# Full TensorE products cut into side-by-side column tiles when narrow tiles ran before them (two-layer transformer block, one core)

## The chip, the cores and the metric

The kernel runs on one core of one Trainium2 chip. The metric is the device time of one execution in microseconds, taken over several runs; one further execution was recorded by the hardware profiler. All data are 32-bit floats.

## The reference

Two layers on an input of 2 sequences x 1024 tokens x 256 features, cut here to what is computed:

```python
# layer 0, attention: 16 query heads of 16, 8 key/value heads, rotary positions
q, k, v = x @ W_Q.T, x @ W_K.T, x @ W_V.T            # x is normalized
scores = einsum('bsdkg,btdk->bkgst', rope(q), rope(k)) / sqrt(256)
ctx = einsum('bkgst,btdk->bkgsd', softmax(scores), v)
attn = ctx @ W_O.T
# layer 0, feed-forward: weights are codes into a table of 16 values
w = lut[idx]                                          # gate, up: 688x256; down: 256x688
ffn = (silu(x @ gate.T) * (x @ up.T)) @ down.T
# layer 1, recurrence per head of 64 (4 heads)
state = (1 - w_t)[..., :, None] * state + k_t[..., :, None] * v_t[..., None, :]
y_t = einsum('bhi,bhij->bhj', r_t, state)             # then y @ Wout
# layer 1, mixture of experts: 8 experts of width 176, two a token, and a shared one of 352
probs = softmax(x @ gate_w.T); weights, selected = top_k(probs, 2)
out = shared(x) + sum over the two of weight * expert(x)
```

Norms, residual products and sums stand around these parts.

## The kernel before

Tokens lie 128 to a partition block (16 blocks) or in four column blocks of 512. Nearly all of the work is on TensorE (PE); VectorE (DVE) takes row maxima, multiplies and masks, ScalarE (ACT) evaluates exponentials and SiLU and copies out of PSUM, GpSimd (POOL) decodes the table weights and does the gathers.

**The order is written out by hand.** `ORDER` is a string of about 2,000 letters. Each letter pops the next step off the list of that letter (`steps`), and each step issues its instructions on all engines. So the order of every engine's queue is fixed by the string. At `>` the attention part ends and its PSUM banks are handed on.

**Three kinds of product**, by how much of the 128x128 array they use:

- *Row tiles*: the contraction is over 32 rows (one head), 128 columns. Scores are computed twice: `largest` (L309, "mx") for the row maxima that DVE reduces (L316), `weigh` (L343, L335, "sc") for the exponentials that ACT takes (L347). Four heads in four row tiles run side by side. In the recurrence `diagonal` (L1192) uses 64 rows, and the second half of `reads` (L1341) 64 rows by 64 columns.
- *Column tiles*: 128 rows, the output in 32 or 64 partitions. `gather` (L371 and L360, "cx") multiplies the exponentials with the values of four heads, in four tiles of 32 columns side by side. `logits` (L728) uses 32 columns, `level` (L1234, "lev"), `states` (L1304) and the first half of `reads` (L1330, "y") use 64.
- *Full products* and transposes: 128 x 128. Full products are `qkv` (L218), `project` (L413, "so"), `gate_up0` (L562, L544, "gu", "gt"), `down0` (L578, "d"), `weights_of_decays` (L633), the recurrence's `project` (L1138), `values` (L1165, "vp") and `result` (L1357), the shared expert's `gate_up_s` (L753, "gus") and `down_s` (L1057, "ds"), the routing's `rank` (L846, L847) and `ids` (L927, "who"), and the experts' `gate_up` (L993) and `down` (L1021).

The kinds alternate often. In attention (about 25 to 560 us) the string mixes m, w (row tiles), v (column tiles), and single steps of the others: transposes (h, j, l, y, p) and full products (f, q, and A, the feed-forward of layer 0). From 567 us on, layer 1's recurrence (r) is woven with the feed-forward, routing (o), the shared expert (s) and the experts (X, G, H, D).

`gate_up_s` works in three blocks of rows of the shared expert's 352: 128, 128 and 96. Its weights `wgs` are loaded on SP's queue (L1096). `ids` collects the token numbers of every expert tile: 16 steps, each fed by a comparison on DVE (L916).

Of the kernel before, what the change touches and what calls it, by code (L numbers as in the profile page):

```python
# [61 lines left out]
NFS = len(FS)  # L62

# [10 lines left out]
C_ALL = C_PRIO + NE  # L74

# [27 lines left out]
def attention(  # L103
    nc, tc, st, b0, small, singles, xs, xnT, s_sb, wlut, ident, epst,
# [24 lines left out]
    for k in range(4):  # L129
        nc.tensor.matmul(bank(f"none_{k}"), xnT[:, 0, 0:P], xnT[:, 0, 0:512], start=True, stop=True)  # L130
# [71 lines left out]
    def turn_x(t):  # L202

        ps = bank(f"xnTp_{t}")
        for kc in range(KC):
            for k in range(2):
                nc.tensor.transpose(
                    ps[:, (2 * kc + k) * P : (2 * kc + k + 1) * P], xns[t + k][:, ts(kc, P)], ident
                )
        nc.scalar.copy(xnT[:, :, t * P : (t + 2) * P], ps.rearrange("p (k s) -> p k s", k=KC))  # L210
# [3 lines left out]
    def qkv(t):  # L214
        b, c = divmod(t, CPB)
        ps = bank(f"qkv_{t}")
        for kc in range(KC):
            nc.tensor.matmul(  # L218
                ps, xnT[:, kc, ts(t, P)], wqkv[:, kc, :], start=(kc == 0), stop=(kc == KC - 1)
            )  # L220
        qk = ps[:, 0:384].rearrange("p (h d) -> p h d", d=8)
        cs = att2.tile([P, 2, 2, HS, 8], F32, tag="cs", name=f"cs_{t}")
        nc.vector.tensor_tensor(
            cs.rearrange("p w a h d -> p w (a h) d"),
            qk.unsqueeze(1).to_broadcast([P, 2, 2 * HS, 8]),
            rope[:, :, c, :].unsqueeze(2).to_broadcast([P, 2, 2 * HS, 8]),
            ALU.mult,
        )
        nc.scalar.copy(vpads[b][:, c, :, 0:HD], ps[:, 384:512].rearrange("p (k d) -> p k d", d=HD))
        turned[t] = cs[:, 0], cs[:, 1]  # L230
# [17 lines left out]
    def turn_k(t):  # L248

        b, c = divmod(t, CPB)  # L250
        pk = bank(f"kTp_{t}")
        pkv = pk.rearrange("p (j k s) -> p j k s", j=2, k=2)
        for j in range(2):
            for k in range(2):
                nc.tensor.transpose(pkv[:, j, k, :], knat[(c + k) % 4][:, ts(j, 4), :], ident)
        nc.scalar.copy(kTs[b][:, :, c * P : (c + 2) * P], pk.rearrange("p (j s) -> p j s", j=2))
# [25 lines left out]
    def turn_q(tag, g, h):  # L282

        b, T = divmod(g, NQT)
        ps = bank(f"{tag}p_{g}_{h}")
        for c in range(BC):
            nc.tensor.transpose(ps[:, ts(c, P)], qns[b][:, T, BC * h + c], ident)
        qT = att2.tile([P, 512], F32, tag=tag, name=f"{tag}_{g}_{h}")
        nc.scalar.copy(qT, ps)
        qTs[tag, g, h] = qT  # L290

    def turn_first(c):

        if c == 0:
            qTs["qTb", 0, 0] = att2.tile([P, 512], F32, tag="qTb", name="qTb_0_0")
        ps = bank(f"qTbp_0_{c}_0")
        nc.tensor.transpose(ps[:, 0:P], qns[0][:, 0, c], ident)
        nc.scalar.copy(qTs["qTb", 0, 0][:, ts(c, P)], ps[:, 0:P])

    def largest(n, i):  # L300

        g, u = divmod(n, 16)
        b, T = divmod(g, NQT)
        c, half = divmod(u, 2)
        if (g, c) not in tops:
            tops[g, c] = att2.tile([P, 2, 4], F32, tag="top", name=f"top_{g}_{c}", bufs=4)
        at = slice(SLOT * i, SLOT * (i + 1))
        ps = bank(f"mx_{n}_{i}")
        nc.tensor.matmul(  # L309
            ps,  # L310
            qTs["qTa", g, c // BC][at, ts(c % BC, P)],
            kTs[b][at, T // 2, ts(half, 512)],
            start=True,
            stop=True,
        )
        nc.vector.tensor_reduce(tops[g, c][:, half, i : i + 1], ps, AX.X, ALU.max)  # L316
        done[g, c] = done.get((g, c), 0) + 1
        if done[g, c] == 8:
            top = tops.pop((g, c))

            nc.vector.tensor_reduce(
                qns[b][:, T, c, :, HD], top.rearrange("p h i -> p i h"), AX.X, ALU.max
            )

    def weigh(n, i):

        g, u = divmod(n, 16)
        b, T = divmod(g, NQT)
        h, c = divmod(u, 8)
        at = slice(SLOT * i, SLOT * (i + 1))  # L330
        ps = bank(f"sc_{n}_{i}")
        if n < 8:

            for k in range(4):
                nc.tensor.matmul(  # L335
                    ps[:, ts(k, P)],
                    kTs[0][at, 0, ts(c % 2 * 4 + k, P)],
                    qTs["qTb", 0, 0][at, ts(c // 2, P)],
                    start=True,
                    stop=True,  # L340
                )
        else:
            nc.tensor.matmul(  # L343
                ps, kTs[b][at, T // 2, ts(c, P)], qTs["qTb", g, h][at, :], start=True, stop=True
            )
        e = att2.tile([P, 512], F32, tag="e", name=f"e_{n}_{i}", bufs=EB)
        nc.scalar.activation(e, ps, AF.Exp, scale=1.0 / math.sqrt(E))  # L347
        es[n, i] = e

    def gather(n):  # L350
# [6 lines left out]
        if n < 8:  # L357
            for k in range(4):
                for i in range(4):
                    nc.tensor.matmul(  # L360
                        cxs[0, 0][SLOT * i : SLOT * (i + 1), ts(c // 2, P)],
                        values(0, c % 2 * 4 + k, i),
                        es[n, i][:, ts(k, P)],
                        start=(c % 2 == 0 and k == 0),
                        stop=(c % 2 == 1 and k == 3),
                    )
        for i in range(4):
            if n < 8:
                es.pop((n, i))
                continue  # L370
            nc.tensor.matmul(  # L371
                cxs[g, h][SLOT * i : SLOT * (i + 1), :],
                values(b, c, 4 * (T // 2) + i),
                es.pop((n, i)),
                start=(c == 0),
# [7 lines left out]
    def divide(g, h):  # L383
# [4 lines left out]
        for c in range(BC):  # L388
            nc.tensor.transpose(ps[:, ts(c, P)], ct[:, ts(c, P)], ident)
# [11 lines left out]
    def turn_c(t):  # L401
        ps = bank(f"cTp_{t}")
        for kc in range(KC):
            nc.tensor.transpose(ps[:, ts(kc, P)], s_sb[:, t, ts(kc, P)], ident)
# [4 lines left out]
    def project(t):  # L409
        cT = cTs.pop(t)  # L410
        po = bank(f"so_{t}")
        for kc in range(KC):
            nc.tensor.matmul(  # L413
# [28 lines left out]
def two_layer_kernel(  # L442
# [69 lines left out]
    def transpose_block(srcs, name):  # L512

        ps = bank2(name)
        for kc in range(KC):
            for k, s in enumerate(srcs):
                nc.tensor.transpose(ps[:, kc, ts(k, P)], s[:, ts(kc, P)], ident)
# [3 lines left out]
    singles = []  # L521
    ffw = ctx.enter_context(ExitStack())
# [16 lines left out]
    def gate_up0(n, f, which):  # L539
        if f == FB:  # L540

            ps = bank1(f"gt0_{n}")
            for kc in range(KC):
                nc.tensor.matmul(  # L544
# [16 lines left out]
        for kc in range(KC):  # L561
            nc.tensor.matmul(  # L562
# [11 lines left out]
    def down0(n, k):  # L574
        t = n * BC + k
        po = bank1(f"d0_{t}")
        for f in range(NF0):
            nc.tensor.matmul(  # L578
# [23 lines left out]
    def late_loads(part):  # L602
# [8 lines left out]
        nc, tc, att, b0, small, singles, xs, xnT, s_sb, wlut, ident, epst,  # L611
# [16 lines left out]
    def weights_of_decays():  # L628
        ps = bank1("wxwp")
        psv = ps.rearrange("p (k d) -> p k d", k=KC)  # L630
        for kc in range(KC):
            for k in range(KC):
                nc.tensor.matmul(  # L633
# [21 lines left out]
    singles.clear()  # L655
    more_hidden(ffw.enter_context(tc.tile_pool(name="h1", bufs=1, side="right")))
# [19 lines left out]
    wgs = shp.tile([P, KC, 2 * SH_CH], F32, name="wgs")  # L676
# [47 lines left out]
    def logits(n):  # L724
        ps = bank1(f"logits_{n}")
        for kc in range(KC):
            for k in range(BC):
                nc.tensor.matmul(  # L728
                    ps[SLOT * k : SLOT * (k + 1), 0:P],
                    gate[:, kc, :],  # L730
                    xnT[:, kc, ts(n * BC + k, P)],
                    start=(kc == 0),
# [15 lines left out]
    def gate_up_s(n, f):  # L748
        lo, sz = FS[f]
        ps = bank2(f"gus_{n}_{f}")  # L750
        for which in range(2):
            for kc in range(KC):
                nc.tensor.matmul(  # L753
                    ps[:sz, which, :],
                    wgs[:, kc, which * SH_CH + lo : which * SH_CH + lo + sz],
# [32 lines left out]
    def top_two(n):  # L788
# [3 lines left out]
        def turn_l():  # L792
            ps = bank1(f"lgp_{n}")
            nc.tensor.transpose(ps[:, 0:P], lgT[n], ident)
# [18 lines left out]
    def route():  # L813
# [29 lines left out]
        def rank():  # L843
            flat = both.rearrange("p c e -> p (c e)")
            ps = bank1("rank")
            nc.tensor.matmul(ps[:, 0:P], before, flat, start=True, stop=True)  # L846
            nc.tensor.matmul(ps[:, P : 2 * P], all1, flat, start=True, stop=True)  # L847
# [75 lines left out]
        def ids(c):  # L923
            if c == 0:
                whop.append(bank1("who"))
            for k in range(2):
                nc.tensor.matmul(  # L927
# [46 lines left out]
    def turn_x(i):  # L974
        ps = bank1(f"xgTp_{i}")
        xg = tiles.pop(("x", i))
        for kc in range(KC):
            nc.tensor.transpose(ps[:, ts(kc, P)], xg[:, ts(kc, P)], ident)
# [7 lines left out]
    def gate_up(i):  # L986
# [5 lines left out]
        for kc in range(KC):  # L992
            nc.tensor.matmul(  # L993
                ps[:, 0 : 2 * EI],
                xT[:, kc, :],
                late["gu"][:, kc, bass.ds(e * (2 * EI), 2 * EI)],
                start=(kc == 0),
# [10 lines left out]
    def turn_h(i):  # L1008
        ps = bank1(f"hgTp_{i}")
        h = tiles.pop(("h", i))  # L1010
        for k in range(2):
            nc.tensor.transpose(ps[:EH, ts(k, P)], h[:, ts(k, EH)], ident)
# [4 lines left out]
    def down(i):  # L1017
        ps = bank1(f"dne_{i}")
        e, hT = tiles.pop(("e", i)), tiles.pop(("hT", i))
        for k in range(2):  # L1020
            nc.tensor.matmul(  # L1021
                ps[:, 0:E],
                hT[:, k, :],
                late["d"][:, k, bass.ds(e * E, E)],
                start=(k == 0),
# [23 lines left out]
    def down_s(n, k, m):  # L1049
# [5 lines left out]
        for c in range(m):  # L1055
            for f, (lo, sz) in enumerate(FS):
                nc.tensor.matmul(  # L1057
# [75 lines left out]
    def project(n, what_):  # L1133
        wt = {"a": wxw, "r": w1[:, :, 0, :], "k": w1[:, :, 1, :]}[what_]
        pp = bank2(f"{what_}p_{n}")
        for m in range(KC):
            for kc in range(KC):
                nc.tensor.matmul(  # L1138
# [19 lines left out]
    def values(n, k):  # L1158
# [4 lines left out]
        for k2 in range(2):  # L1163
            for kc in range(KC):
                nc.tensor.matmul(  # L1165
# [15 lines left out]
    def diagonal(n, m):  # L1181
# [7 lines left out]
        for c in range(BC):  # L1189
            for par in range(2):  # L1190
                at = half(par)
                nc.tensor.matmul(  # L1192
# [13 lines left out]
    def level(n, lev):  # L1206
# [11 lines left out]
        for c in range(BC):  # L1218
            for pr in range(KC):
                for hf in range(2):  # L1220
# [10 lines left out]
                    else:  # L1231
                        continue
                    w_ = P if m == HALF else HALF
                    nc.tensor.matmul(  # L1234
                        ps[half(at), w_ * q : w_ * (q + 1)], kd[:, pr, src], to, start=True, stop=True
# [45 lines left out]
    def turn_k(n):  # L1281
        kd = B_[n, "k"]
        pt = bank2(f"kTp_{n}")
        for c in range(BC):
            for m in range(KC):
                nc.tensor.transpose(
# [8 lines left out]
    def states(n):  # L1295
# [4 lines left out]
        for c in range(BC):  # L1300
            for m in range(KC):
                for par in range(2):
                    ch = slice(P * m + 64 * par, P * m + 64 * (par + 1))
                    nc.tensor.matmul(  # L1304
                        puv[half(par), c, m, :], ke[:, c, ch], v[:, c, ch], start=True, stop=True
# [16 lines left out]
    def reads(n):  # L1322
# [3 lines left out]
        for c in range(BC):  # L1326
            for m in range(KC):
                for par in range(2):
                    ch = slice(P * m + 64 * par, P * m + 64 * (par + 1))
                    nc.tensor.matmul(  # L1330
                        pyv[half(par), m, c, :],
                        v[:, c, ch],
                        w[:, c, m, par, :],
                        start=(c == 0),
                        stop=False,
                    )
        for c in range(BC):
            for m in range(KC):
                for par in range(2):
                    at = half(par)  # L1340
                    nc.tensor.matmul(  # L1341
# [10 lines left out]
    def result(n, k):  # L1352
        po = bank1(f"s1_{n}_{k}")
        pov = po.rearrange("p (k d) -> p k d", k=2)
        for k2 in range(2):
            for m in range(KC):
                nc.tensor.matmul(  # L1357
# [110 lines left out]
def _arrays(i):  # L1468
# [27 lines left out]
    gs = np.concatenate([i["L1_ffn_shared_gate"], i["L1_ffn_shared_up"]], axis=0)  # L1496
# [43 lines left out]
```

## Time and profile before

| | us |
|---|---|
| median of 3 runs | 968.42 |
| lowest, highest | 968.21, 970.19 |
| the profiled execution | 968.03 |
| its span, from the first to the last instruction | 966.2 |

| stretch | what runs | PE busy | DVE busy |
|---|---|---|---|
| 0 to 100 us | norms, qkv, attention begins | 97.26 of 100 | 83.46 |
| 200 to 300 us | attention | 100.00 of 100 | 73.93 |
| 500 to 567 us | end of attention, feed-forward | 67.00 of 67 | 9.52 |
| 567 to 745 us | feed-forward, recurrence, routing, shared expert | 176.47 of 178 | 109.38 |
| 745 to 905 us | experts, recurrence | 159.40 of 160 | 74.40 |

How to read it: an engine's busy time is the union of its instructions' durations. Matmuls are pipelined, so the durations of neighbours overlap, and the time that a matmul costs the next one is the difference of their starts. "PEld" is the load of the stationary operand, which may run beside a matmul. A row of the timeline merges neighbouring instructions of one line and shape: start, length, engine, line, operation, output<-inputs, rows*columns of the array, and the count.

### The profile page before, as it was taken

What the parts mean: (1) busy time and instruction counts of PE and PEld (TensorE: products, weight loads), DVE (VectorE), ACT (ScalarE), POOL (GpSimd) and SP (SyncE); (2) the same over time, 40 slices, a digit from 0 to 9 for tenths busy, and PEclk for the clock granted to TensorE, in tenths of its full rate; (3) what the DMA queues carried; (4) which work ended last, traced back from release to release, by engine and by line L of the source; (5) the groups of instructions that cost most, each with busy time, mean ns of one, the idle gap of its engine ahead of it and who ended that gap; (6) DMA issues with size and microseconds to landing.
All of it is one profiled execution on the core that took longest, in us unless ns stands there. A gap on an engine that the chain in (4) does not pass through costs nothing.

```text
span 966.2 us, 17253 instructions
## 1 busy us (share of the span) xinstructions
PE 946.4 (98%) x6716; PEld 521.3 (54%) x6716; DVE 612.9 (63%) x1228; ACT 533.6 (55%) x1009; POOL 586.9 (61%) x485
## 2 busy tenths in 40 slices
PE   9999999999999999999999999999999999999976
PEld 4685433343334443443445475756457678777765
DVE  6998886877767766765760134467777634641795
ACT  4556856566675775766677545526313553464223
POOL 8999999999999999999912030202002345553244
PEclk9999999999999999999999999999999999999999
DMA  5000000000000000000000031002600122221142
GB/s 177 2 2 13 1 12 2 1 13 1 12 2 1 12 1 13 1 1 1 1 1 1 1 124 40 25 1 77 191 1 26 47 67 66 67 80 53 56 141 95
DMA packets 17864, 34.53 MB, mean 36 GB/s; under 512 B 2893, under 2 KB 11231, under 8 KB 17439
## 3 DMA queue, kind: packets, MB, share of 16 engines
q1 hardware_dynamic: 13527, 21.96, 7.2%
q0 software_dynamic: 3968, 10.80, 3.6%
q8 instruction: 54, 0.88, 0.4%
q10 hardware_dynamic: 288, 0.66, 0.2%
q14 instruction: 27, 0.22, 0.1%
HBM read 22.01 MB, written 11.40 MB: 35 GB/s over the span
## 4 chain that ended last, share of the span: by engine, by line
PE 93%; DVE 4%; issue 1%; POOL 1%; ACT 0%; POOLq 0%; ACTq 0%; DVEq 0%
PE sc L343 15%; PE mx L309 14%; PE cx L371 12%; PE gu L562 7%; PE gue L993 5%; PE d L578 4%; PE gus L753 4%; PE dne L1021 3%; PE qkv L218 3%; PE lev L1234 3%; PE sc L335 2%; PE so L413 2%; PE rp L1138 1%; PE vp L1165 1%; PE kp L1138 1%
## 5 line engine op out<-in xcount | busy, mean ns | idle before, releaser
L316 DVE TENSOR_REDUCE top<-mx 128x1 f32<-128x512 f32 x512 | 325.9, 684 | 100.1 <-PE mx L309 66.3
L347 ACT ACTIVATE e<-sc 128x512 f32<-128x512 f32 x512 | 271.7, 605 | 133.3 <-PE sc L343 61.4
L309 PE MATMUL mx<-kT,qTa 32*128 32x512 f32 x1024 | 282.7, 625 | 0.3 <-DVE top L316 0.3
L270 POOL TENSOR_SCALAR pick<-idx,lut 128x544 f32<-128x544 int32 x120 | 252.4, 2103 | 11.3
L343 PE MATMUL sc<-qTb,kT 32*128 32x512 f32 x960 | 254.8, 624 | 0.0
L274 POOL TENSOR_TENSOR wlut<-wlut,pick 128x544 f32<-128x544 f32 x120 | 160.5, 1337 | 10.0
L309 PEld LDWEIGHTS mx<-kT,qTa 32*128 32x128 f32 x1024 | 102.5, 183 | 63.3 <-DVE top L316 23.7
L343 PEld LDWEIGHTS sc<-qTb,kT 32*128 32x128 f32 x960 | 93.5, 183 | 76.6 <-DVE top L316 24.4
L371 PE MATMUL cx<-e,vpad 128*32 128x512 f32 x960 | 123.9, 603 | 0.0
L588 POOL TENSOR_TENSOR sgt<-s_sb,g 128x256 f32<-128x256 f32 x16 | 11.6, 728 | 154.0 <-ACT g L586 154.0
L966 POOL DMA_INDIRECT xg<-xn_h,who x39 | 39.4, 1009 | 94.8 <-PE s L1357 70.2
L1034 POOL DMA_INDIRECT y_h<-ye,who x39 | 39.8, 1021 | 69.3 <-ACT ye L1029 23.8
L562 PE MATMUL gu<-xnT,wlut 128*128 128x512 f32 x160 | 72.8, 598 | 0.0
L371 PEld LDWEIGHTS cx<-e,vpad 128*32 128x32 f32 x960 | 20.8, 108 | 84.1 <-issue 72.8
L1005 DVE TENSOR_TENSOR sge<-sge,gue 128x176 f32<-128x176 f32 x39 | 13.1, 338 | 73.4 <-ACT sge L1004 73.1
L572 DVE TENSOR_TENSOR h<-sg,gu 128x512 f32<-128x512 f32 x20 | 13.8, 688 | 65.5 <-ACT sg L571 50.3
L993 PE MATMUL gue<-wgu,xT 128*128 x156 | 53.0, 462 | 1.5 <-issue 0.9
L562 PEld LDWEIGHTS gu<-xnT,wlut 128*128 128x128 f32 x160 | 29.2, 190 | 34.0 <-issue 29.9
L578 PE MATMUL d<-wlut,h 128*128 128x256 f32 x192 | 44.1, 381 | 0.5 <-ACT s_sb L416 0.5
L753 PE MATMUL gus<-xnT,wgs 128*128 128x512 f32 (+1 forms) x96 | 43.1, 598 | 0.0
L1021 PE MATMUL dne<-wd,hTe 88*128 x156 | 40.0, 381 | 0.5 <-ACT hTe L1014 0.5
L578 PEld LDWEIGHTS d<-wlut,h 128*128 128x128 f32 x192 | 35.7, 190 | 8.1 <-issue 1.8
(235 smaller groups left out, 1330.3 us busy)
## 6 DMA issues: line engine op xcount, KB each, us to landing
xn_h<-xn SPq DMA_DIRECT2D x16, 256.0 KB, 3.6
yk<-y_h SPq DMA_DIRECT2D x16, 256.0 KB, 2.9
wgu<-in_wgu SPq DMA_DIRECT2D x1, 2816.0 KB, 10.3
idx<-in_idx SPq DMA_DIRECT2D x8, 272.0 KB, 2.8
out_x<-g SPq DMA_DIRECT2D x16, 128.0 KB, 1.7
wd<-in_wd SPq DMA_DIRECT2D x1, 1408.0 KB
xs<-in_x SPq DMA_DIRECT2D x2, 512.0 KB, 5.0
w<-in_w SPq DMA_DIRECT2D x1, 1024.0 KB
```

The lines of the kernel that those rows point to most:

```text
L270: nc.gpsimd.tensor_scalar(dst, codes[piece], float(j), lut[:, j : j + 1], ALU.is_equal, ALU.mult)
L274: nc.gpsimd.tensor_tensor(wlut[:, at], wlut[:, at], dst, ALU.add)
L309: nc.tensor.matmul(ps, qTs["qTa", g, c // BC][at, ts(c % BC, P)], kTs[b][at, T // 2, ts(half, 512)], start=True, stop=True,)
L316: nc.vector.tensor_reduce(tops[g, c][:, half, i : i + 1], ps, AX.X, ALU.max)
L343: nc.tensor.matmul(ps, kTs[b][at, T // 2, ts(c, P)], qTs["qTb", g, h][at, :], start=True, stop=True)
L347: nc.scalar.activation(e, ps, AF.Exp, scale=1.0 / math.sqrt(E))
L371: nc.tensor.matmul(cxs[g, h][SLOT * i : SLOT * (i + 1), :], values(b, c, 4 * (T // 2) + i), es.pop((n, i)), start=(c == 0), stop=(c == CPB ...
L562: nc.tensor.matmul(hT0[which], wlut[:, lo + kc * P :][:, 0:P], xnT[:, kc, ts(n, 512)], start=(kc == 0), stop=(kc == KC - 1),)
L578: nc.tensor.matmul(po[:, 0:E], hidden(n)[:, f, ts(k, P)], wd0[:, f, :], start=(f == 0), stop=(f == NF0 - 1),)
L753: nc.tensor.matmul(ps[:sz, which, :], wgs[:, kc, which * SH_CH + lo : which * SH_CH + lo + sz], xnT[:, kc, ts(n, 512)], start=(kc == 0), s ...
L993: nc.tensor.matmul(ps[:, 0 : 2 * EI], xT[:, kc, :], late["gu"][:, kc, bass.ds(e * (2 * EI), 2 * EI)], start=(kc == 0), stop=(kc == KC - 1),)
L1021: nc.tensor.matmul(ps[:, 0:E], hT[:, k, :], late["d"][:, k, bass.ds(e * E, E)], start=(k == 0), stop=(k == 1),)
```

## The change

A small class now issues the products and keeps the width of the last column tile in `form` (SLOT is 32, HALF 64, P 128):

```diff
+class Array:
+    def __init__(self, nc, narrow):
+        self.nc, self.narrow, self.form = nc, narrow, None
+
+    def rows(self, out, lhsT, rhs, start=True, stop=True):
+        self.form = None
+        self.nc.tensor.matmul(out, lhsT, rhs, start=start, stop=stop)
+
+    def matmul(self, out, lhsT, rhs, start, stop, width=None):
+        if len(lhsT.shape) > 2:
+            lhsT = lhsT.rearrange("p a b -> p (a b)")
+        w = self.form = width or self.form or self.narrow
+        for i in range(0, out.shape[0], w):
+            self.nc.tensor.matmul(out[i : i + w], lhsT[:, i : i + w], rhs, start=start, stop=stop)
+
+    def transpose(self, out, in_, ident):
+        self.form = P
+        self.nc.tensor.transpose(out, in_, ident)
```

All products go through it. Row tiles (L309, L335, L343, L1192, L1341) call `te.rows`, transposes call `te.transpose`, and the others call `te.matmul`. Column tiles give their own width, so they are issued as before; the experts' two products and the first four dummy products (L130) give `width=P` and stay full. The rest of the full products give none: each becomes four instructions of 32 columns, two of 64, or stays one, by what was issued last.

```diff
+    te = Array(nc, SLOT)
...
     go(">")
     att.close()
     singles.clear()
+    te.narrow, te.form = HALF, None
...
-        nc.tensor.matmul(
+        te.rows(
             ps,
             qTs["qTa", g, c // BC][at, ts(c % BC, P)],
             kTs[b][at, T // 2, ts(half, 512)],
...
-            nc.tensor.matmul(
+            te.matmul(
                 cxs[g, h][SLOT * i : SLOT * (i + 1), :],
                 values(b, c, 4 * (T // 2) + i),
                 es.pop((n, i)),
+                width=SLOT,
                 start=(c == 0),
...
-            nc.tensor.matmul(
+            te.matmul(
                 ps, xnT[:, kc, ts(t, P)], wqkv[:, kc, :], start=(kc == 0), stop=(kc == KC - 1)
             )
...
-                nc.tensor.matmul(
+                te.matmul(
                     whop[0][:, 0:NTILE],
                     at[c][:, k, :],
                     inside[:, 2 * c + k, :],
...
-            nc.tensor.matmul(
+            te.matmul(
                 ps[:, 0 : 2 * EI],
                 xT[:, kc, :],
                 late["gu"][:, kc, bass.ds(e * (2 * EI), 2 * EI)],
+                width=P,
```

The third block of `gate_up_s`, 96 rows wide before, is computed 128 wide, so that tiles divide it; its weights get 32 columns more, of zeros at the end, and the extra rows of the product are not read.

```diff
+SH_PAD = NFS * P - SH_CH
...
-    wgs = shp.tile([P, KC, 2 * SH_CH], F32, name="wgs")
+    wgs = shp.tile([P, KC, 2 * SH_CH + SH_PAD], F32, name="wgs")
...
-                nc.tensor.matmul(
-                    ps[:sz, which, :],
-                    wgs[:, kc, which * SH_CH + lo : which * SH_CH + lo + sz],
+                te.matmul(
+                    ps[:, which, :],
+                    wgs[:, kc, which * SH_CH + lo : which * SH_CH + lo + P],
                     xnT[:, kc, ts(n, 512)],
```

`ORDER`, the tiles, the pools and all instructions of the other engines are unchanged.

## The prediction

> **What bounds the kernel now.** I read the page first: busy shares and the chain of work that ended last.
>
> ```profile
> span 966.2 us, 17253 instructions
> PE 946.4 (98%) x6716; PEld 521.3 (54%) x6716; DVE 612.9 (63%) x1228; ACT 533.6 (55%) x1009; POOL 586.9 (61%) x485
> PE   9999999999999999999999999999999999999976
> PE 93%; DVE 4%; issue 1%; POOL 1%; ACT 0%; POOLq 0%; ACTq 0%; DVEq 0%
> ```
>
> TensorE (PE) is busy in every slice but the last two, and 93% of the closing chain is its own matmuls. So a saving on PE is worth its length almost everywhere, and only the end needs another look. A busy PE need not be streaming, though, so the second view is the timeline of TensorE, where differences of start times count (durations overlap).
>
> ```profile
> 98.86 1.07 PE L371 MATMUL cx<-e,vpad 128*32 128x512 f32 x8
> 99.86 1.99 PE L218 MATMUL qkv<-wqkv,xnT 128*128 128x512 f32 x4
> 101.77 1.07 PE L371 MATMUL cx<-e,vpad 128*32 128x512 f32 x8
> ...
> 576.30 13.90 PE L562 MATMUL gu<-xnT,wlut 128*128 128x512 f32 x32
> 590.12 0.64 PE L728 MATMUL logits<-xnT,gate 128*32 128x128 f32 x16
> ```
>
> The pair before the types is rows*columns of the array in use: 128*128 is a full product, 128*32 a tile of 32 columns, 32*128 a tile of 32 rows (mx, sc). One call shows as two matmuls, "passes" below (gu has 80 calls and 160 matmuls). A long run of full passes takes (590.12 - 576.30 = 13.82) / 32 = 0.43 us each. Four narrow ones run side by side: cx x8 is two rounds of four. But 99.86 to 101.77 is 1.91 us for four full passes worth 4 x 0.429 = 1.72, and cx x8 takes 1.00 us for two rounds worth 0.86. The rest, 0.19 and 0.14 us, is lost at changes of shape.
>
> From the starts of single matmuls that loss has two parts. **The change**: first start of the new shape less the last start of the old and its streaming time lies between 85 and 105 ns at 375 of the 390 changes, whatever the pair of shapes; I use 95. **The entry**: the second pass of the new shape comes later than in a steady run, by 104 ns for full products of 256 to 512 columns (533 against 429), 55 for transposes, 21 for the 39-column "who", 105 for row tiles, 24 for four narrow tiles (453 against 429), 50 for two.
>
> **The change, part by part.** I went through the 6,716 matmuls in order of start and gave each the shape that the new rule gives it (a row-tile product clears the form, a transpose sets it to full, a narrow product sets its width, a full product takes the form it finds, or 32, later 64, where there is none). Of the 988 full-product passes 116 become four tiles of 32 columns, 340 two tiles of 64, 532 stay full, all those behind a transpose among them.
>
> Changes of shape: 390 before, 360 after. The 30 fewer save 30 x 95 = 2.85 us.
> Entries before: 34 full products at 104, 61 transposes at 55, 3 "who" at 21, 111 four-tile at 24, 33 two-tile at 50, 4 of 64*64 at 50, 144 row tiles at 105: 26.6 us. After: 3, 68, 0, 115, 26, 4 and 144: 23.4 us. That saves 3.16 us. Transposes are entered seven times more, because a narrow product ahead of one now has to be left.
> Together 6.0 us: 2.8 before 567 us, 1.4 from 567 to 745, 0.3 from 745 to 905, 1.5 after it.
>
> **A saving on short products.** Weight loads bound small passes:
>
> ```profile
> 730.23 1.08 PE L927 MATMUL who<-inside,at 128*128 128x39 f32 x8
> 731.24 1.97 PE L1330 MATMUL y<-w,v 128*64 128x128 f32 x32
> 733.14 0.65 PE L1341 MATMUL y<-rd,zero 64*64 64x128 f32 x8
> ...
> 618.57 1.16 PE L1234 MATMUL lev<-rd,kT 128*64 128x64 f32 x32
> 619.66 0.70 PE L1165 MATMUL vp<-w,x2T 128*128 128x256 f32 x2
> ```
>
> "who" takes 1.01 us for 8 passes, 112 ns each in the middle, though it streams only 39 columns. lev takes 1.09 us for 16 rounds of two tiles, 58 ns a round. 48 of the 64 "who" passes become rounds of two tiles, which no row shows with 39 columns. Bounds: 112 ns each (no gain), 58 as lev (gain 48 x 54 = 2.6 us). lev is the nearer row, having the same width of load. But the matches that feed "who" come from DVE one by one, and the x16 run near 727 us shows PE idle for them, so 1.6 us of the 2.6 is taken as reaching the end.
>
> **What the narrow passes cost.** A row shows four tiles of 32 columns in steady state: from cx x32 to cx x64 eight more rounds of 128 columns cost 1.88 - 1.01 = 0.87 us, 109 ns each, exactly a full pass of 128.
>
> ```profile
> 55.32 1.08 PE L360 MATMUL cx<-e,vpad 128*32 128x128 f32 x32
> 56.33 1.14 PE L309 MATMUL mx<-kT,qTa 32*128 32x512 f32 x8
> 57.40 1.96 PE L360 MATMUL cx<-e,vpad 128*32 128x128 f32 x64
> 59.28 0.71 PE L309 MATMUL mx<-kT,qTa 32*128 32x512 f32 x3
> ```
>
> y above does the same for two tiles: 1.90 us for 16 rounds, 109 each plus change and entry. Four or two tiles that read one and the same moving tile, and two tiles with 256 or 512 columns, are in no row. Bounds: nothing a pass (those two rows), or 24 ns a pass, the delay that the second round has behind an entry, if weights were never loaded ahead: 456 x 24 = 10.9 us. I take nothing, since the shortest of these rounds, 128 columns, already hides its loads.
>
> Issue was my next doubt. lev starts 32 matmuls in 1.09 us, 34 ns each, and the four of a cx round start within 21 ns. [...]
>
> **Edits at no cost.** 688 more matmuls and as many loads lengthen PE's instruction stream by a tenth; instruction fetching takes 0.4% of the DMA engines (queue q8), which covers it; uncovered, the rows above would show starved rounds. Semaphores: cx signals on the last matmul of its eight alone, so tiles should add none. The last block of gus widens from 96 to 128 columns; its load goes from 159 to 190 ns under a pass of 429. wgs grows by 32 KB on SP's queue (in front of msk and wds); the load is issued at 570 us and gus first runs at 657, so 87 us cover it. No step is moved.
>
> **What of it reaches the end.** Until 567 us PE waits for data in few places; POOL decodes weights until 488 us and the first "d" that needs all of them starts at 512, so 24 us of slack lie there. DVE is 65 to 83% busy in the 100 us windows. I count 2.5 of the 2.8. From 567 to 745: 1.3 of 1.4. From 745 to 905, PE 99.6% busy: 0.3. After 905 it is different:
>
> ```profile
> 905.00:940.00 35.00, 28.16 (x270) 22.73 (x269) 33.47 (x54) 6.01 (x15) 10.90 (x12) 1.00 0.37 118
> 940.00:944.00 4.00, 4.00 (x16) 3.30 (x15) 3.93 (x9) 1.14 (x3) 2.34 (x2) 0.57 0.32 104
> ```
>
> These are windows: PE, its loads, DVE, ACT, POOL, granted clock, DMA. The timeline of TensorE in them:
>
> ```profile
> 925.38 1.15 PE L1234 MATMUL lev<-rd,kT 128*64 128x64 f32 x32 [1.60 <-DVE kT L1247]
> 938.91 1.09 PE L1234 MATMUL lev<-rd,kT 128*64 128x128 f32 x16 [3.14 <-DVE kT L1247]
> 939.94 3.31 PE L1165 MATMUL vp<-w,x2T 128*128 128x256 f32 x8
> ```
>
> Until 940 us DVE is busy for 33.5 of 35 us and PE waits for it, so a faster ds or vp is only a longer wait: 0.2 of 1.5.
>
> Sum: 2.5 + 1.3 + 1.6 + 0.3 + 0.2 = 5.9 us. The profiled execution took 968.03 us (span 966.2, 1.8 around it), 0.4 under the median of 968.42; 968.03 - 5.9 = 962.1, and against the median **962.5 us**.
>
> **Rivals.**
> (1) Other engines take the gain. For: DVE above 70% in attention, matches behind "who". If attention keeps 0.8, 567 to 745 keeps 0.7 and "who" and the end nothing: 1.8 us with the 0.3, so 966.6. Against: at 375 of 390 changes the next shape follows at once, without a wait.
> (2) Narrow passes are slower. Mechanism: tiles that share one moving tile, or that cannot load ahead, pay 24 ns on each of 456 passes: 10.9 - 5.9 = 5.0 us slower, 973.4. It decides from 5.9 / 456 = 13 ns a pass. For: no row has shared moving tiles, and cx runs hold more than two rounds of 512 rarely. Against: where they do (303.58 us, x16), later rounds take 429.
> (3) More arrives. All of 2.8 and 1.4 and 2.6 and 0.3, 0.7 of the end, and the clock dip at 940.5 to 943.9 misses vp (3.31 us at half clock, 1.99 for the same eight passes at 926): 9.1 us, so 959.3. The dip follows an idle stretch of 3.14 us, which earlier ds passes lengthen; so it may as well stay. [...]
>
> **How the numbers follow.** Forecast 0.60, rival 1 0.14, rival 2 0.14, rival 3 0.12. A measurement of this kernel tells about 0.2%, 1.9 us, from no change. The forecast and rival 3 are faster (0.72), rival 1 lies within it (0.14), rival 2 is slower (0.14). The range runs from below rival 3, with "who" and attention in full, 957.5, to half-way into rival 2, at 17 ns a pass (456 x 17 = 7.8, less 5.9, 970.3).
>
> **What would show it.** In the new timeline, qkv between two cx at 99 us should be x16 matmuls of 128*32, with 8 rounds from the first cx to the next mx in 3.55 us instead of 3.91. gu behind cx should still take 0.43 a pass; 0.45 is rival 2. "who" should start pairs every 58 ns. At 567 us the same d should start 2 to 3 us earlier; if not, rival 1. The forecast is wrong if passes lengthen, if each tile signals or waits, or if the gain at 905 us is gone at the end.

## The result, and the profile after

The changed kernel takes 962.98 us (median of 4 runs, 962.56 to 963.91), the kernel before 969.12 on the same chip (4 runs, 968.21 to 970.19): a ratio of 0.9939, with a 95% interval of 0.9927 to 0.9951. The forecast was 962.5. The profiled execution took 962.75 us, 5.28 less than the one before.

The page of the changed kernel, its span, busy shares and chain of waits:

```profile
span 961.0 us, 18629 instructions
PE 939.6 (98%) x7404; PEld 499.9 (52%) x7404; DVE 615.0 (64%) x1228; ACT 533.7 (56%) x1009; POOL 586.8 (61%) x485
PE 93%; DVE 5%; issue 1%; POOL 1%; ACT 0%; POOLq 0%; ACTq 0%; DVEq 0%
```

688 matmuls more (7,404 against 6,716), as counted, and still the same bound: TensorE (PE) busy for 98%. TensorE's busy time fell by 6.8 us, but that number can't say why. The timeline of TensorE can (L88 issues row tiles, L95 all other products, L99 transposes):

```profile
99.11 1.06 PE L95 MATMUL cx<-e,vpad 128*32 128x512 f32 x8
100.00 1.90 PE L95 MATMUL qkv<-wqkv,xnT 128*32 128x512 f32 x16
101.71 1.04 PE L95 MATMUL cx<-e,vpad 128*32 128x512 f32 x8
102.69 0.69 PE L88 MATMUL sc<-qTb,kT 32*128 32x512 f32 x1
...
722.84 2.24 PE L95 MATMUL who<-inside,at 128*128 128x39 f32 x16 [0.34 <-DVE at L946]
725.01 1.15 PE L95 MATMUL add<-v,ke 128*64 128x64 f32 x32
725.99 0.62 PE L95 MATMUL who<-inside,at 128*64 128x39 f32 x16
726.43 1.95 PE L95 MATMUL y<-w,v 128*64 128x128 f32 x32
...
933.59 1.50 PE L95 MATMUL lev<-rd,kT 128*64 128x128 f32 x16 [3.21 <-DVE kT L1279]
934.87 3.22 PE L95 MATMUL vp<-w,x2T 128*64 128x256 f32 x16
938.14 1.09 PE L99 MATMUL kTp<-cst,kT 128*128 128x128 f32 x8
```

Before, the row tiles behind the second cx started here:

```profile
102.77 0.69 PE L343 MATMUL sc<-qTb,kT 32*128 32x512 f32 x1
```

Three things are to be seen. The qkv that stood between two cx as x4 of 128*128 is now x16 of 128*32, and from the first cx to the next sc 3.58 us pass, where it was 3.91 (98.86 to 102.77; 3.55 forecast): both changes of shape are gone, and four qkv rounds take 1.71 us, 0.43 each. The narrow who takes 0.44 us for eight rounds from its start to that of y, where it took 1.01 us before, a change of shape included. And near the end TensorE still waits 3.21 us for DVE ahead of the last lev, and vp still runs at half clock (3.22 us; the window 934.0 to 937.5, shown under "Fillers", has a granted clock of 0.52).

Over the whole trace the count of changes of shape is 360 (390 before), as forecast. Of these, 348 still cost 85 to 105 ns by the prediction's measure (375 of the 390 before). Rounds of four tiles start every 429 ns at 512 columns and every 216 at 256, rounds of two every 429, 216 and 58 at 512, 256 and 39 columns (medians), as full passes of 512 and 256 columns did. The tiles signal no more often than the full products did: qkv 16 times and gu 28 times in both traces.

**Where the time came from.** A matmul that both kernels issue in the same shape is a landmark: its start before less its start after is the lead of the changed kernel. The table has the starts of five landmarks in the traces of all kernels run, in us: the first row tile of attention (mx), the first transpose of layer 1 (x1Tp), a transpose of an expert's tokens (xgTp), the last of the experts' products (dne) and a product of the recurrence near the end (lev).

| kernel | first mx | first x1Tp | third tile's xgTp | last tile's dne | last lev of 128 columns | end |
|---|---|---|---|---|---|---|
| before | 25.64 | 572.83 | 746.31 | 908.69 | 938.91 | 966.24 |
| changed | 25.88 | 570.84 | 741.23 | 903.27 | 933.59 | 960.97 |
| all full | 26.86 | 574.12 | 747.70 | 910.07 | 940.30 | 968.85 |
| attention only | 25.85 | 570.77 | 744.35 | 906.73 | 936.97 | 964.39 |
| layer 1 only | 26.81 | 574.09 | 744.43 | 906.47 | 936.80 | 965.26 |
| always narrow | 25.90 | 574.79 | 746.59 | 908.62 | 938.92 | 966.16 |
| who full | 26.08 | 571.01 | 743.37 | 905.42 | 935.75 | 964.00 |
| ds full | 26.88 | 571.80 | 742.11 | 904.15 | 934.41 | 961.08 |
| with fillers | 26.08 | 570.96 | 741.32 | 903.35 | 933.69 | 960.18 |
| best | 26.66 | 571.41 | 740.83 | 902.87 | 933.17 | 959.64 |

Until the first mx only full products and transposes run, and they are issued alike in all kernels but "always narrow" and "best". Still the first column scatters by 1.2 us. Most of that is there already behind the dummy products, whose eight passes took 5.53 us before and 6.76 in "all full". So leads below are counted from the first mx. The changed kernel gains 2.23 us to x1Tp (1.99 and the 0.24 of a later start), 3.09 from there to xgTp, 0.34 from there to dne, and gives back 0.15 by the end. With the 0.24 of the start that is 2.23 + 3.09 + 0.34 - 0.15 - 0.24 = 5.27 of span.

### The profile page after: what moved, and what is told of

It reads as the page before. It is cut to its first block, busy times and chain, and to the rows that moved or that the text cites. A ratio compares the mean times of both kernels' runs of the same rounds, so it can differ in the third digit from the quotient of the medians.

```text
span 961.0 us, 18629 instructions
## 1 busy us (share of the span) xinstructions
PE 939.6 (98%) x7404; PEld 499.9 (52%) x7404; DVE 615.0 (64%) x1228; ACT 533.7 (56%) x1009; POOL 586.8 (61%) x485
## 4 chain that ended last, share of the span: by engine, by line
PE 93%; DVE 5%; issue 1%; POOL 1%; ACT 0%; POOLq 0%; ACTq 0%; DVEq 0%
PE sc L88 17%; PE mx L88 14%; PE cx L95 13%; PE gu L95 7%; PE gue L95 5%; PE d L95 4%; PE gus L95 4%; PE dne L95 3%; PE qkv L95 3%; PE lev L95 2%; PE so L95 2%; PE kp L95 1%; PE ap L95 1%; PE rp L95 1%; DVE w L1304 1%
## 5 line engine op out<-in xcount | busy, mean ns | idle before, releaser
L88 PE MATMUL mx<-kT,qTa 32*128 32x512 f32 x1024 | 283.1, 625 | 0.3 <-DVE top L341 0.3
L88 PE MATMUL sc<-qTb,kT 32*128 32x512 f32 (+1 forms) x1216 | 282.5, 552 | 0.0
L88 PEld LDWEIGHTS sc<-qTb,kT 32*128 32x128 f32 x1216 | 119.1, 184 | 78.4 <-DVE top L341 24.9
L88 PEld LDWEIGHTS mx<-kT,qTa 32*128 32x128 f32 x1024 | 102.4, 183 | 63.9 <-DVE top L341 23.9
L95 PE MATMUL cx<-e,vpad 128*32 128x512 f32 (+1 forms) x1216 | 132.1, 533 | 0.0
L95 PEld LDWEIGHTS cx<-e,vpad 128*32 128x32 f32 x1216 | 27.9, 108 | 86.3 <-issue 74.0
L95 PE MATMUL gu<-xnT,wlut 128*32 128x512 f32 (+2 forms) x320 | 72.1, 592 | 0.0
L95 PE MATMUL gue<-wgu,xT 128*128 x156 | 53.0, 462 | 1.6 <-issue 1.0
L95 PE MATMUL d<-wlut,h 128*128 128x256 f32 (+2 forms) x300 | 43.8, 379 | 0.5 <-ACT s_sb L443 0.5
L95 PEld LDWEIGHTS gu<-xnT,wlut 128*32 128x32 f32 (+2 forms) x320 | 25.1, 137 | 36.2 <-issue 35.1
L95 PE MATMUL gus<-xnT,wgs 128*64 128x512 f32 (+2 forms) x184 | 42.8, 593 | 0.0
L95 PE MATMUL dne<-wd,hTe 88*128 x156 | 40.0, 380 | 0.5 <-ACT hTe L1045 0.5
L1273 DVE TENSOR_TENSOR rd<-rd,up 128x512 f32<-128x512 f32 x48 | 33.2, 732 | 9.0 <-PE lev L95 9.0
```

Of the source, the lines that this page charges most:

```text
L88: self.nc.tensor.matmul(out, lhsT, rhs, start=start, stop=stop)
L95: self.nc.tensor.matmul(out[i : i + w], lhsT[:, i : i + w], rhs, start=start, stop=stop)
L1273: nc.vector.tensor_tensor(rv[:, par, :, 1, :], rv[:, par, :, 1, :], dec[:, :, 0:1].to_broadcast([P, q, m]), ALU.mult,)
```

## Experiments

The theory, as in the prediction: the gain is the changes of shape that are gone, the cheaper entries, and the shorter loads of who. The rivals: narrow products are quicker in themselves, by their shorter loads; or the gain comes from something beside them, such as the padding.

**All full** and the two halves. The one line that picks the width, in three kernels:

```diff
-        w = self.form = width or self.form or self.narrow
+        w = self.form = width or P
...
+        w = self.form = width or (P if self.narrow == HALF else self.form or self.narrow)
...
+        w = self.form = width or (P if self.narrow == SLOT else self.form or self.narrow)
```

> Every full product that gives no width stays one instruction of 128 columns; the padded third block of gus stays. Accounting theory (the gain is fewer and cheaper changes of shape, and shorter loads of who): 390 changes as before and no gain, so the time of before within 0.1% (969), and the start of any matmul within 0.3 us of before's. Rival (padding or the new class does part of it): some us away from before.

> Narrow full products in attention only (to 567 us), full ones after it. Accounting theory: 378 changes, TensorE about 2.0 us ahead of before at 567 us as in the changed kernel, and still about 2.0 ahead at 905 us; total 966.9 to 967.2. Rival (other engines catch up later): the lead shrinks after 567 us and the total is that of before.

> Full products whole in attention, narrow after it. Accounting theory: 372 changes, no lead at 567 us, 3.1 at 745, 3.4 at 905, total 965.6 to 966; together with the attention-only kernel the leads add to the 5.4 of the changed kernel. Rival: the leads do not add, since a layer 1 that starts later or earlier meets its DMAs and DVE differently.

Measured: all full 968.11 us, ratio to before 0.9997 (0.9988 to 1.0006); attention only 966.96, 0.9980 (0.9971 to 0.9989); layer 1 only 966.79, 0.9970 (0.9958 to 0.9982). In the table, counted from the first mx, "all full" stays within 0.2 us of before up to the last lev, so neither the class nor the padding does anything that these traces show. In absolute starts it missed the 0.3 us expected, since its first mx came 1.22 us late. "Attention only" is 2.27 us ahead at x1Tp and still 2.17 at xgTp and dne: nothing downstream takes the lead back, and the total lies in the 966.9 to 967.2 expected. "Layer 1 only" is level at x1Tp, 3.05 ahead at xgTp and 3.39 at dne. The two add to 2.17 + 3.39 = 5.56 at dne, and the changed kernel has 5.66. So the leads of the parts add, to within 0.1 us. The total of "layer 1 only" missed the 965.6 to 966 expected. Its trace shows where: the last lev is 3.28 us ahead, but from there to the end 28.46 us pass, 27.33 before. There lev and vp both run at half clock: from the start of that lev to that of kTp 5.32 us pass, where before, with 3.4 us at half clock, took 4.13. Its one run at a mean granted clock of 0.998 took 964.04 us; the six at 0.995 took 965.31 to 967.13.

**Always narrow**: a transpose no longer sets the form.

```diff
     def transpose(self, out, in_, ident):
-        self.form = P
         self.nc.tensor.transpose(out, in_, ident)
```

> A transpose no longer sets the form, so full products behind a transpose are narrow too. Accounting theory: 410 changes; by the prices of the prediction 1.8 us behind before at 567 us (2.76 ahead by the same count for the changed kernel, so 4.6 apart), 1.0 or so gained from 567 to 745, about the time of before at the end, 967 to 970. Rival (narrow products are quicker in themselves, by their shorter loads): more narrow passes, more gain, below 960.

Measured: 969.07 us, 1.000 (0.9992 to 1.0009). It has 8,336 matmuls, 410 changes, and less weight-load time (PEld 477.0 us busy, 499.9 in the changed kernel, 521.3 before), and the gain is gone. Its rounds are as quick as in the changed kernel (429, 216 and 58 ns at 512, 256 and 39 columns), so narrow products are not slower; but more of them bring no more gain, which is the opposite of what products quicker in themselves would give. Its timeline:

```profile
99.54 1.06 PE L95 MATMUL cx<-e,vpad 128*32 128x512 f32 x8
100.42 1.90 PE L95 MATMUL qkv<-wqkv,xnT 128*32 128x512 f32 x16
102.14 1.04 PE L95 MATMUL cx<-e,vpad 128*32 128x512 f32 x8
103.11 0.69 PE L88 MATMUL sc<-qTb,kT 32*128 32x512 f32 x1
...
566.63 1.48 PE L95 MATMUL d<-wlut,h 128*32 128x256 f32 x24
567.92 1.05 PE L95 MATMUL so<-wo,cT 128*32 128x256 f32 x16
569.46 5.40 PE L95 MATMUL d<-wlut,h 128*64 128x256 f32 x48 [0.49 <-ACT s_sb L442]
574.79 1.09 PE L98 MATMUL x1Tp<-cst,xn 128*128 128x128 f32 x8
```

Where a narrow neighbour stands beside it, qkv gains as in the changed kernel (3.57 us from cx to sc). Where transposes do, each narrow product is entered and left for nothing. Counted from the first mx it is 1.70 us behind before at x1Tp, where the prices of the prediction, applied to its order, give 2.1 (the 1.8 expected were for 567 us), and 0.33 ahead at dne, its gains in layer 1 included.

**Who full**: the routing's short product goes back to one tile.

```diff
                     inside[:, 2 * c + k, :],
+                    width=P,
```

> The changed kernel with who (ids) given width 128, so its 48 narrow passes are full again, and so is what follows it up to the next narrow product. Accounting by the prices: 2.9 us less gain between 706 and 745 us if TensorE set that stretch; DVE's matches set part of it (1.9 of 3.1 us arrived), so 1.5 to 2 us: TensorE's lead over before at 769 us 3.4 to 3.9 instead of 5.4, total 964.5 to 965. Rival (who is bound by DVE, the lead there came from the changes of shape around it): lead at 769 us 4.8 or more.

Measured: 964.81 us, 0.9959 (0.9945 to 0.9973). The lead at dne from the first mx is 3.71 us against 5.66, so who and the three changes that come back with it (0.3 us by count) are worth 1.95 us of the 2.9 that the prices give. At xgTp it is 3.38, against the 3.4 to 3.9 expected at 769 us. The total lies in the expected range only as a median between two groups, three runs at 963.8 to 963.9 us and three at 965.7 to 965.9; the lead is the test. So the shorter passes of who count (a pair every 58 ns for one every 112; medians of one load are 0.138 us for 64 columns, 0.192 for 128), and about a third of the saving does not arrive. Part of that third is a wait for DVE's matches, which neither this kernel nor before has and the changed one has. Before, and then the changed kernel:

```profile
715.26 1.09 PE L1234 MATMUL lev<-rd,kT 128*64 128x128 f32 x16
716.29 1.08 PE L927 MATMUL who<-inside,at 128*128 128x39 f32 x8
```

```profile
711.42 1.07 PE L95 MATMUL lev<-rd,kT 128*64 128x128 f32 x16
712.91 0.77 PE L95 MATMUL who<-inside,at 128*64 128x39 f32 x16 [0.41 <-DVE at L946]
```

The rest of the third is not located.

**Ds full**: the shared expert's last product, which stands among the waits near the end, goes back to one tile.

```diff
                     wds[:sz, f, :],
+                    width=P,
```

> The changed kernel with the shared expert's last product (ds) given width 128: nine changes of shape come back after 905 us, 1.6 us of TensorE time. Theory (DVE sets the end from 905 us on): the leads at 905 and at lev near 933 us stay within 0.1 us of the changed kernel's, total within 0.5 us of 963 but for the clock. Rival (they count): 1 us or more later at 933.

Measured: 963.01 us, 0.9943 (0.9930 to 0.9956), no slower than the changed kernel. That alone would not settle it, since the two profiled executions differ in their starts (1.0 us) and in the half clock near the end, which "ds full" had not. The lead does: from the first mx to the last lev 907.53 us pass, 907.71 in the changed kernel. In the timeline of TensorE the nine changes are back and lost in waits for DVE:

```profile
928.41 1.13 PE L95 MATMUL ds<-wds,xnT 128*128 128x256 f32 x4 [0.59 <-ACT v L1205]
929.38 0.60 PE L95 MATMUL ds<-wds,hS 96*128 96x256 f32 x2
929.81 1.03 PE L95 MATMUL ds<-wds,xnT 128*128 128x256 f32 x4
930.68 0.60 PE L95 MATMUL ds<-wds,hS 96*128 96x256 f32 x2
934.41 1.09 PE L95 MATMUL lev<-rd,kT 128*64 128x128 f32 x16 [3.13 <-DVE kT L1280]
```

**Fillers**: five products whose result is overwritten fill the two long waits of the last block.

```diff
         ps = bank1(f"lev_{n}_{lev}")
+        if n == NBLK - 1:
+            for _ in range({4: 2, 6: 3}.get(lev, 0)):
+                te.matmul(
+                    ps, ident, w1[:, 0, 0:2, :].rearrange("p a d -> p (a d)"), start=True, stop=True, width=HALF
+                )
```

> The changed kernel with five extra products (identity by weights, overwritten afterwards) in the two waits of TensorE ahead of lev 4 and lev 6 of the last block, 1.7 and 2.6 us long in waits of 1.8 and 3.2. Theory (the half clock at 934 us follows the idle stretch): no half clock before the end, vp's eight passes in 1.9 us instead of 3.2, the end 1.2 us earlier, total 961.7 and less scatter. Rival: the dip stays, or the fillers delay lev, no gain or a loss.

Measured: 962.00 us, 0.9935 (0.9922 to 0.9947). Windows of the same place, with TensorE, loads, DVE, ACT, POOL, granted clock and DMA, in the changed kernel:

```profile
934.00:937.50 3.50, 3.50 (x28) 2.41 (x25) 3.19 (x6) 0.42 (x1) 2.07 (x2) 0.52 0.37 112
```

and with the fillers, then TensorE's timeline there:

```profile
934.00:937.50 3.50, 2.65 (x33) 1.77 (x28) 3.46 (x7) 1.00 (x2) 1.96 (x2) 1.00 0.38 114
```

```profile
930.30 2.74 PE L95 MATMUL lev<-w,cst 128*64 128x512 f32 x12
933.69 1.09 PE L95 MATMUL lev<-rd,kT 128*64 128x128 f32 x16 [0.64 <-DVE kT L1284]
934.62 1.90 PE L95 MATMUL vp<-w,x2T 128*64 128x256 f32 x16
937.36 1.09 PE L99 MATMUL kTp<-cst,kT 128*128 128x128 f32 x8 [0.84 <-DVE kT L1284]
```

The clock stays full and vp takes 1.90 us, not 3.22. The end comes 26.49 us after the last lev, 27.38 in the changed kernel: 0.9 us won of the 1.2 expected, because kTp now waits 0.84 us for DVE. The two kernels' intervals overlap, so the ratio does not show the gain; the trace shows it for one execution. "Ds full" had no half clock there either, without fillers: its vp took 1.90 us behind a wait of 3.13. So the trace with fillers does not show that they are what kept the clock full. The smaller scatter that was expected is not shown: five runs lie within 0.6 us, the sixth took 963.43 at a mean clock of 0.996.

**Best**: the fillers, who always as two tiles of 64 with three buffers for its matches, and the second sequence's norms on ACT.

```diff
-        rt_two = rtp.enter_context(tc.tile_pool(name="route2", bufs=2))
+        rt_two = rtp.enter_context(tc.tile_pool(name="route2", bufs=3))
...
                     inside[:, 2 * c + k, :],
+                    width=HALF,
...
-        if t < CPB:
-            nc.scalar.activation(xn, xs[:, t, :], AF.Identity, bias=mvs[t], scale=rstds[t])
-        else:
-            nc.vector.tensor_scalar(xn, xs[:, t, :], mvs[t], rstds[t], ALU.subtract, ALU.mult)
+        nc.scalar.activation(xn, xs[:, t, :], AF.Identity, bias=mvs[t], scale=rstds[t])
```

(the negated mean that ACT needs is then made for both sequences)

> The fillers, who always two tiles of 64 with three buffers for DVE's matches instead of two, and the norms of the second sequence on ACT instead of DVE (DVE's one took 0.42 to 1.27 us beside POOL). Expected against the changed kernel: 1.2 us from the fillers, 0.3 to 0.9 from who, 0.3 to 0.8 from the norms up to 170 us if ACT has room; total 959.5 to 961. Rival: the norms delay ACT's exponentials, and the lead at 200 us is smaller than the changed kernel's.

Measured: 961.26 us, 0.9922 (0.9908 to 0.9935), the fastest of all medians, and just above the 959.5 to 961 expected. From the first mx it leads before by 2.44 us at x1Tp (changed kernel 2.23), 6.50 at xgTp (5.32), 7.62 at the end (5.51). Read by stretch, that is 0.2 for the norms, below the 0.3 to 0.8 expected, 1.0 for who, above its 0.3 to 0.9, and 0.9 for the end. The three edits were not run apart, so these shares rest on the stretches alone. In TensorE's timeline the x16 of who that took 2.17 us at 722.84 (from its start to the next) now takes 1.26 us:

```profile
723.39 1.44 PE L95 MATMUL who<-inside,at 128*64 128x39 f32 x32 [0.34 <-DVE at L942]
724.65 1.13 PE L95 MATMUL add<-v,ke 128*64 128x64 f32 x32
```

The wait of 0.34 us ahead of it is still for DVE.

## Why the prediction was right

**The prices were right.** A change of 95 ns and an entry by shape, summed over the order, give the lead at x1Tp as 2.5 us (2.23 came) and for "layer 1 only" from xgTp to dne 0.34 (0.34 came). They also gave the sign of the kernel that is narrow everywhere and its size to 0.4 us. They were furthest off for "attention only", 2.76 by the prices at x1Tp and 2.27 measured.

**Full speed in narrow shape** was the choice between two bounds, 0 and 24 ns a pass. It is 0: tiles that share one moving tile stream as fast as cx did (429 ns a round of 512 columns). Rival 2 needed 13 ns a pass and falls. A pair of tiles with 39 columns starts every 58 ns here, and a four-tile round of 256 columns every 216. So two tiles are issued within 58 ns and four within 216, and the doubt about issue falls too.

**Attention**: 2.5 forecast, 2.23 measured. The 2.5 was 2.8 by the prices, less 0.3 for which the prediction gives no working; that this guess came close is luck. The trace shows one place that takes 0.33. DVE's timeline, before and after, each with POOL's:

```profile
149.32 0.42 DVE L199 TENSOR_SCALAR xn<-xs,mv_a,rstd_a 128x256 f32<-128x256 f32 x1
149.67 2.58 DVE L316 TENSOR_REDUCE top<-mx 128x1 f32<-128x512 f32 x4
```

```profile
148.25 1.34 POOL L274 TENSOR_TENSOR wlut<-wlut,pick 128x544 f32<-128x544 f32 x1
149.69 2.10 POOL L270 TENSOR_SCALAR pick<-idx,lut 128x544 f32<-128x544 int32 x1
```

```profile
149.18 0.74 DVE L224 TENSOR_SCALAR xn<-xs,mv_a,rstd_a 128x256 f32<-128x256 f32 x1
149.84 2.58 DVE L341 TENSOR_REDUCE top<-mx 128x1 f32<-128x512 f32 x4
```

```profile
148.42 1.35 POOL L299 TENSOR_TENSOR wlut<-wlut,pick 128x544 f32<-128x544 f32 x1
149.87 2.10 POOL L295 TENSOR_SCALAR pick<-idx,lut 128x544 f32<-128x544 int32 x1
```

DVE comes 0.14 us earlier, POOL 0.17 later, and the same norm takes 0.74 us instead of 0.42. In both it ends 0.15 us after POOL's TENSOR_TENSOR has. The row maxima behind it, which TensorE's mx needs for its banks (its load waits 0.73 us for them, 0.40 before), start 0.17 us later instead of 0.14 earlier, and the lead in absolute starts falls from 0.15 to -0.18 there. That DVE waited for POOL is inferred from these ends; no run shows it apart, or what would make it wait. Not every norm beside POOL takes longer: in the changed kernel the one that starts 0.88 us into POOL's TENSOR_SCALAR of 137.03 takes 0.41 us and ends 0.82 us ahead of it. With the norms on ACT, tried only within the "best" kernel, attention gains 0.2 us more.

**567 to 745 us**: 1.3 + 1.6 = 2.9 forecast, 3.09 measured. The discount on who was right in kind and about right in size: with who full 1.95 us go, of 2.9 by the prices. Its size was a judgement, though, and the x16 run near 727 us that the prediction gave as its reason stands behind a transpose and stays full in the changed kernel; the wait that came is at the who of 712.91.

**After 905 us**: 0.2 forecast, -0.15 measured from dne on, of 1.5 counted. DVE sets the end, as its 33.97 us of the 35 from 905 to 940 say, and "ds full" shows it: 1.6 us of changes back, none in the time. Rival 3's missed dip of the clock did not come in the profiled execution of the changed kernel; the dip stayed and vp took 3.22 us, 3.31 before.

**Rival 1** (other engines take the gain) holds where the forecast had put it, behind who and at the end, and at the one norm in attention. Nothing takes the lead of attention back later: "attention only" keeps 2.17 of its 2.27 us to dne.

The sum missed by 0.6 us of span: 0.27 short in attention, 0.35 short at the end and 0.24 from a later start of that execution, against 0.2 more than forecast from 567 to 905 us. No large errors cancel.

## What to carry to other kernels

Where narrow tiles and full products alternate, sum two prices over the order that the engine really runs: so much for each change of array shape (95 ns here), and so much for the entry, by the shape entered (21 to 105 ns here). In these traces a full product cut into side-by-side tiles cost nothing extra in streaming (429 ns for 512 columns either way), so it paid to cut it where its neighbours were narrow and to leave it whole where they were not. A rule that looks only at what ran before did well here; cutting everywhere lost the gain. The one product that streams fewer columns than it loads (39 against 128) started every 112 ns as one tile and every 58 as two, and most of that saving arrived, as far as its inputs came in time.

## What was not expected of the hardware

The time of one kernel scatters in steps: beside the experiments, before's runs at a mean granted clock of 0.995 took 969.93 to 970.50 us, those at 0.997 and 0.998 took 967.34 to 968.46. In the changed kernel's trace the granted clock is half for 3.413 us from 934.13 us on, behind the wait of 3.21 us that ended at 933.59, then full for 20.48 us, then half to the end. The trace of before has the same lengths: half for 3.413 us from 940.46 on, behind the wait of 3.14 us that ended at 938.91, then full for 20.48.

What followed a wait for DVE ahead of lev differs between traces. The length of vp behind it shows the clock: 1.90 us in two tiles and 1.99 in one where it stayed full.

| kernel | wait, us | ended at | behind it |
|---|---|---|---|
| before | 1.60 | 925.38 | full clock (1.00 from 905 to 940), vp 1.99 |
| before | 3.14 | 938.91 | half clock for 3.41 us, vp 3.31 |
| changed | 1.80 | 920.02 | full clock, vp 1.90 |
| changed | 3.21 | 933.59 | half clock for 3.41 us, vp 3.22 |
| all full | 1.60 | 926.78 | vp 1.99 |
| all full | 3.14 | 940.30 | granted clock of 0.62 from 938 to 947: 6.8 us at half |
| layer 1 only | 1.83 | 923.23 | vp 1.90 |
| layer 1 only | 3.21 | 936.80 | lev and vp at half clock, vp 3.63 |
| always narrow | 1.81 | 925.37 | vp 3.42, granted clock of 0.66 from 925 to 930: 3.4 us at half |
| always narrow | 2.88 | 938.92 | vp 3.56 |
| who full | 1.80 | 922.18 | vp 1.90 |
| who full | 3.19 | 935.75 | lev and vp at half clock, vp 3.63 |
| ds full | 1.61 | 920.88 | vp 1.90 |
| ds full | 3.13 | 934.41 | vp 1.90 |

So in these traces the length of the wait does not settle it. After 1.81 us the clock fell in one kernel and after 1.83 it stayed in another; after 3.13 us it stayed, and after 3.14 it was half for 3.4 us in one and 6.8 in another. What does settle it is not shown. With the fillers the last wait was 0.64 us, and the granted clock was 1.00 from 905 to 940 us.

The start adds its own 1.2 us: the first mx comes between 25.64 and 26.88 us in kernels that begin with the same instructions.
